# Turned weights moved in 2 KB runs and a newly planned order, in a four-layer graph stack on one core

## The chip, the cores and the metric

One core of a Trainium2 chip runs the kernel. The metric is device time in microseconds (us), the median of the timed runs; lower is better. Three runs of the kernel before took 3433.74, 3434.24 and 3435.35 us. The profile is of one further execution.

## The reference, cut to what matters

The input is `x` of 32 samples, each with 512 nodes and 256 channels, in float32, and one 512 x 512 adjacency matrix. Four layers follow one another, and after each one `x = layernorm(x + layer(x))`:

```
a: h = x W;  e = leaky(s1[i] + s2[j]);  softmax over neighbours;  elu(attention @ h)      one head
b: q, k, v;  8 heads of softmax(mask(q k^T)) @ v;  layernorm;  feed-forward;  layernorm
c: as a, with 4 heads of 64 channels
d: e = leaky((x W1)(x W2)^T);  masked softmax;  relu(attention @ (x W3))
```

All four build 512 x 512 attention weights row by row: the softmax runs along a row, with the node `i` on the partitions. To multiply them with the values they must be turned, so that the summed-over node `j` lies on the partitions. How they are turned for two heads of layer c is what the change is about.

## The kernel before, in words

Every sample is a graph of some 450 operations. `Plan.op` records an operation with its engine, its assumed duration, the buffers that it writes, reads and takes, and a stage name: the layer's letter and a digit (0 prepares, 1 makes scores and masks, 2 finishes the layer, 3 is softmax and turning, 4 is weighting). `Plan.order` then plans one instruction order for all engines: a list scheduler that holds up to four samples in flight (`WINDOW = 4`) and picks, for each free engine, the ready operation with the least key, `o.graph * AGE[e] - o.rank - URGENT[e].get(o.stage, 0)`. For TensorE the key gets `SWITCH_WEIGHT` times a penalty from the table `SWITCH`, for taking an operation of another form than the last one. The engines then run this order strictly, and semaphores hold them to the dependencies. So a change of `AGE`, `URGENT` or `SWITCH_WEIGHT` moves every instruction of the program and adds none.

TensorE has three forms of work. **Full**: matmuls and transposes on the whole 128 x 128 array. **Rows** (L934): the scores of layer b, four heads side by side, each on 32 of the array's rows. **Columns** (L603, in `weighted`): the weighting in b (four heads on 32 columns each) and in c (two heads on 64 columns each). A stretch of one form, from a change of form to the next, is called a run of that form below.

Each float32 matmul is two MATMUL records in the trace; a transpose is one. One group of four row heads is 8 records; one weighting of b is 32 records, one of c is 16.

Turning is done in two ways. In most places `turn` (L586) lets TensorE transpose four 128 x 128 blocks into a PSUM bank, which ScalarE or VectorE copies out (L529, L531) to a `pq` buffer. For heads 2 and 3 of layer c, in all but the last two samples (`BY_TRANSFERS`, `PLAIN`), TensorE is spared: the four row blocks of a head lie in one tile `tq`; VectorE transposes each 32 x 32 square in place (L702, STREAM_TRANSPOSE), and 16 transfers, issued by SyncE (SP) at L714, move the squares to their places in `pq`. Those are 60 heads, with 240 in-place transposes and 960 transfers of 64 KB. A transfer takes 32 partitions to 32 others, as 16 pieces of 32 floats (128 bytes) per partition. The other users of SP are the loads (L358) and the stores of the result (L1108).

Buffers are counted: 16 of `t` (one row block each), 2 of `tq`, 5 of `pq`, 8 PSUM banks.

Of the kernel before, what the change touches and what calls it, by code (L numbers as in the profile page):

```python
# [39 lines left out]
AGE = {"PE": 257, "ACT": 221, "DVE": -182, "POOL": 528, "SP": 151}  # L40
URGENT = {
    "PE": {"a0": -75, "a1": 707, "a2": 344, "b0": -756, "b1": 306, "b2": 700, "c0": -1085, "c1": -566, "c2": -26, "d0": -1544, "d1": -1472, "d2": -1512, "a3": 1865, "a4": 679, "b3": 269, "b4": -122, "c3": 3149, "c4": 468, "d3": -1054, "d4": 94},
    "ACT": {"a0": -877, "a1": 23, "a2": 412, "b0": 1122, "b1": 150, "b2": 22, "c0": 432, "c1": -809, "c2": -763, "d0": 680, "d1": -1928, "d2": -1182, "a3": 920, "a4": 701, "b3": 234, "b4": -604, "c3": 1629, "c4": 1505, "d3": -786, "d4": -337},
    "DVE": {"a0": 633, "a1": 670, "a2": 648, "b0": 1045, "b1": -236, "b2": -513, "c0": -2048, "c1": -657, "c2": 497, "d0": -1572, "d1": -869, "d2": -2025, "a3": 1551, "a4": 544, "b3": -1617, "b4": -331, "c3": 91, "c4": 1954, "d3": -1641, "d4": -1168},
    "POOL": {"a0": -1566, "a1": -815, "a2": 2482, "b0": 1576, "b1": -742, "b2": -986, "c0": -744, "c1": -1896, "c2": 3131, "d0": 1272, "d1": 1709, "d2": -1760, "a3": -1181, "a4": 746, "b3": -824, "b4": 1874, "c3": -105, "c4": 2168, "d3": 1794, "d4": 2316},
    "SP": {"a0": 578, "a1": -291, "a2": 1436, "b0": -478, "b1": -110, "b2": -662, "c0": -380, "c1": -1000, "c2": 35, "d0": 1115, "d1": -375, "d2": -249, "a3": 144, "a4": 71, "b3": -603, "b4": 627, "c3": -231, "c4": 1331, "d3": 989, "d4": -515},
# [6 lines left out]
SWITCH_WEIGHT = 869  # L53
# [18 lines left out]
class Buf:  # L72
# [13 lines left out]
    def place(self, tiles, words):  # L86
        if self.tag is None:
            self.view = self.pool.tile(self.shape, self.dtype, tag=self.name, name=self.name, bufs=1)
            return
        name = f"{self.tag}_{self.slot}"  # L90
        if name not in tiles:
            tiles[name] = self.pool.tile([self.shape[0], words], F32, tag=name, name=name, bufs=1)
        view = tiles[name][:, 0 : self.words()]
        if self.dtype != F32:
            view = view.bitcast(self.dtype)
        if len(self.shape) > 2:
            dims = " ".join("abc"[: len(self.shape) - 1])
            sizes = {k: n for k, n in zip("abc", self.shape[1:])}
            view = view.rearrange(f"p ({dims}) -> p {dims}", **sizes)
        self.view = view  # L100
# [210 lines left out]
def gnn_stack(  # L311
# [31 lines left out]
    def buf(tag, shape, name, cells=1, dtype=F32):  # L343
        return Buf(work, shape, tag, BUFS[tag], name, cells, dtype)
# [155 lines left out]
    class Rows:  # L500


        def __init__(self, buf, cell=None):
            self.buf, self.cell = buf, cell
            self.use = buf if cell is None else (buf, cell)

        def __call__(self):
            return self.buf[:] if self.cell is None else self.buf[:, self.cell]

    def rows(n, name, together=False):  # L510

        if together:
            t = buf("tq", [P, n, N], name, n)
            return [Rows(t, i) for i in range(n)]
        return [Rows(buf("t", [P, N], f"{name}_{i}")) for i in range(n)]
# [64 lines left out]
    def turn(t, pT, pcell, to, name):  # L580
# [3 lines left out]
        def issue(e):  # L584
            for j in range(NB):
                nc.tensor.transpose(ps[:, j], t()[:, block(j)], ident)  # L586

        op({PE: 0.44}, issue, [ps], [t.use], [pT])
        copied(N, to, lambda: ps[:], [(pT, pcell)], [ps])

    def weighted(pv, oT, pTs, of, v, lo, D, us):
# [4 lines left out]
        def issue(e):  # L596
            for j in range(NB):
                for h in range(P // D):
                    p = of(h, j)
                    at = pv[h * D : (h + 1) * D]  # L600
                    if len(p.shape) > 2:
                        at = at.rearrange("d (i n) -> d i n", n=P)
                    nc.tensor.matmul(  # L603
# [76 lines left out]
    def masked(s, t, top, i):  # L680


        def issue(e):
            nc.vector.tensor_tensor_reduce(  # L684
                out=t(), in0=s[:], in1=neg[:, i], scale=1.0, scalar=LOWEST, op0=ALU.add,
# [3 lines left out]
        op({DVE: 0.61}, issue, [t.use, (top, i)], [s, (neg, i)])  # L689

    def turned(ts, pT, blocks, by_transfers, name):


        if not by_transfers:
            for i in blocks:
# [3 lines left out]
            return  # L699

        for i in blocks:
            op({DVE: FLIP_US}, lambda e, t=ts[i]: nc.vector.transpose(t(), t()), [ts[i].use], [])  # L702
        t = ts[0].buf

        def squares():
            return t[:].rearrange("p i (j n) -> p (i j) n", n=P)

        for a in range(P // SQ):

            def move(e, a=a):  # L710
                here = slice(a * SQ, (a + 1) * SQ)
                for b in range(P // SQ):
                    there = slice(b * SQ, (b + 1) * SQ)
                    nc.sync.dma_start(out=pT[there, :, here], in_=squares()[here, :, there])  # L714

            op({SP: P // SQ * DMA_US}, move, [(pT, a)], [t], lag=2.0)

    def leaky_softmax(ts, top, v, src, total, at, blocks, name):
# [17 lines left out]
        for i in blocks:  # L736

            def leaky(e, i=i, t=ts[i]):
                nc.scalar.activation(  # L739
                    t(), t(), AF.Prelu, alpha=SLOPE,  # L740
# [3 lines left out]
            def exp(e, i=i, t=ts[i]):  # L744
                nc.scalar.activation(  # L745
                    t(), t(), AF.Exp, bias=bias[:, i : i + 1],
# [3 lines left out]
            op({ACT: 0.53 if src is None else 0.62}, leaky, [ts[i].use], [] if src is None else [v])  # L750
            op({ACT: 0.71}, exp, [ts[i].use, (total, at * NB + i)], [bias])
# [30 lines left out]
    class Gat(Layer):  # L782
# [31 lines left out]
        def attend(self):  # L814
            H, D, name, v = self.H, C // self.H, self.name, self.v
            G = min(H, P // D) if H > 1 else 1
            for g in range(0, H, G):
# [3 lines left out]
                for h in range(G):  # L821
                    plan.stage = name[0] + "1"
                    dst = bank([P, N], f"{name}_dst{g}{h}")
                    by_transfers = (
                        g + h in BY_TRANSFERS[name[0]] and int(name[1:]) < B - PLAIN
                    )
                    ts = rows(NB, f"{name}_t{g}{h}", by_transfers)
                    pT = buf("pq", [P, NB * NB, P], f"{name}_pT{g}{h}", NB)
# [8 lines left out]
                    o = op({PE: 0.44}, issue, [dst], [v], [t.buf for t in ts])  # L837
# [6 lines left out]
                    turned(ts, pT, range(NB), by_transfers, f"{name}_{g}{h}")  # L844
# [3 lines left out]
                if H > 1:  # L848
# [4 lines left out]
                        lambda h, j, pTs=pTs: pTs[h][:].rearrange(  # L853
                            "p (i j) n -> p i j n", j=NB
                        )[:, :, j],
# [34 lines left out]
    def rows_weighted(pv, pT, v, y, f):  # L890

        for i in range(FB):

            def issue(e, i=i):
                for j in range(NB):
                    nc.tensor.matmul(  # L896
                        pv[:, i], lhsT=pT[:, (f * FB + i) * NB + j], rhs=v[:, j, 0:C],
# [3 lines left out]
            reads = pT if BY_TRANSFERS[y.name[0]] else (pT, f * FB + i)  # L901
            op({PE: 1.73}, issue, [pv], [reads, v], [y])

    class Transformer(Layer):
# [14 lines left out]
        def attend(self):  # L919
            name, q_sb, k_sb = self.name, self.q, self.k  # L920
            for f in range(F):
# [4 lines left out]
                for c in range(NC):  # L926
                    ts = [rows(Q, f"{name}_t{f}{c}{i}") for i in range(FB)]
                    for i in range(FB):
                        ss = [bank([P, N], f"{name}_s{f}{c}{i}{q}") for q in range(Q)]

                        def scores(e, i=i, ss=ss, c=c, f=f):
# [8 lines left out]
                            {PE: 0.95}, scores, ss, [(q_sb, f), k_sb], [t.buf for t in ts[i]],  # L940
                            form="rows",
                        )
                        for q in range(Q):
# [3 lines left out]
                            def reduce(e, i=i, h=h, t=t, s=s, f=f, low=low):  # L947
                                nc.vector.tensor_tensor_reduce(  # L948
                                    out=t(), in0=s[:], in1=neg[:, f * FB + i],
# [4 lines left out]
                            def exp(e, i=i, h=h, t=t, low=low, total=total):  # L954
                                nc.scalar.activation(  # L955
                                    t(), t(), AF.Exp, bias=low[:, i, h : h + 1], scale=-1.0,
# [4 lines left out]
                            op({DVE: 0.61}, reduce, [t.use, (low, cell)], [s, (neg, f * FB + i)])  # L961
                            op({ACT: 0.71}, exp, [t.use, (total, cell)], [(low, cell)])

                    pTs = [
                        buf("pq", [P, 2 * NB, FN], f"{name}_pT{f}{c}{k}", 2 * FB)
                        for k in range(Q // 2)
                    ]
                    plan.stage = name[0] + "3"
                    for i in range(FB):
                        for q in range(Q):  # L970
                            pT, lo = pTs[q // 2], q % 2 * NB
                            turn(
                                ts[i][q], pT, q % 2 * FB + i,
                                lambda pT=pT, lo=lo, i=i: pT[:, lo : lo + NB, block(i)],
                                f"{name}_tr{f}{c}{i}{q}",
                            )
# [4 lines left out]
                        lambda h, j, pTs=pTs: pTs[h // 2][:, h % 2 * NB + j],  # L981
# [61 lines left out]
    class Bilinear(Layer):  # L1043
# [13 lines left out]
        def attend(self):  # L1057
            name, hh, xT = self.name, self.hh, self.xT
            ts = rows(NB, f"{name}_t", bool(BY_TRANSFERS["d"]))
            pT = buf("pq", [P, NB * NB, P], f"{name}_pT", NB)  # L1060
            top = tiny("top", [P, NB], f"{name}_top", NB)
            total = tiny("total", [P, NB, 1], f"{name}_total", NB)
            for f in range(F):
# [3 lines left out]
                for i in blocks:  # L1067
# [9 lines left out]
                    op({PE: 1.73}, issue, [s], [(hh, f), xT], [ts[i].buf])  # L1077
# [3 lines left out]
                turned(ts, pT, blocks, False, f"{name}_{f}")  # L1081
# [5 lines left out]
                plan.stage = name[0] + "4"  # L1087
                pv = bank([P, FB, C], f"{name}_pv{f}")
                y = self.part_y(f)
                rows_weighted(pv, pT, self.v, y, f)  # L1090

                def issue(e, y=y, pv=pv, inv=inv):
                    for i in range(FB):
                        nc.vector.tensor_scalar(
                            y[:, i], pv[:, i], inv[:, i], 0.0, ALU.mult, ALU.max
                        )

                op({DVE: 0.79}, issue, [y], [pv, inv])
                plan.stage = name[0] + "1"
                yield f  # L1100
# [97 lines left out]
```

## Time and profile before

| what | value | how to read it |
|---|---|---|
| timed runs | 3434.24 us median of 3 | device time |
| span of the profiled execution | 3429.9 us | first to last instruction; 4.3 us less than the median of the timed runs |
| TensorE (PE) busy | 3397.8 us, 99% | ends of matmuls are modelled, so busy is not peak |
| VectorE (DVE) busy | 2922.9 us, 85% | |
| ScalarE (ACT) busy | 2785.3 us, 81% | |
| GpSimd (POOL) busy | 854.4 us, 25% | |
| transfers through SP's queue | 563,456 packets, 117.98 MB | 16.0% of 16 DMA engines' span |
| granted TensorE clock | 0.999 of full speed | mean over the span |

The profile has a view by group of instructions (busy time, mean, idle time before), one of waits (who waited for whom), the chain of work that ended last (at each step: what released it, with its duration), a timeline, and a table of busy time by stretch. A line number in it is that of the kernel printed above.

### The profile page before, as it was taken

What the parts mean: (1) busy time and instruction counts of PE and PEld (TensorE: products, weight loads), DVE (VectorE), ACT (ScalarE), POOL (GpSimd) and SP (SyncE); (2) the same over time, 40 slices, a digit from 0 to 9 for tenths busy, and PEclk for the clock granted to TensorE, in tenths of its full rate; (3) what the DMA queues carried; (4) which work ended last, traced back from release to release, by engine and by line L of the source; (5) the groups of instructions that cost most, each with busy time, mean ns of one, the idle gap of its engine ahead of it and who ended that gap; (6) DMA issues with size and microseconds to landing.
All of it is one profiled execution on the core that took longest, in us unless ns stands there. A gap on an engine that the chain in (4) does not pass through costs nothing.

```text
span 3429.9 us, 65651 instructions
## 1 busy us (share of the span) xinstructions
PE 3397.8 (99%) x22744; PEld 2531.6 (74%) x22744; DVE 2922.9 (85%) x8645; ACT 2785.3 (81%) x6747; POOL 854.4 (25%) x840
## 2 busy tenths in 40 slices
PE   8999999999999999999999999999999999999998
PEld 6766777777777777777777777777777777777766
DVE  7889888888888888898888888888888889888886
ACT  6788788888788888888787888878888888878785
POOL 1222132222222222222223222222222222222322
PEclk9999999999999999999999999999999999999999
DMA  2012111121121220112211112102122011221100
GB/s 95 11 26 44 30 28 36 40 44 37 20 43 33 44 44 18 39 32 44 44 31 26 37 39 44 38 19 44 32 44 44 18 39 32 44 44 31 26 20 19
DMA packets 563787, 122.17 MB, mean 36 GB/s; under 512 B 510848, under 2 KB 562688, under 8 KB 563456
## 3 DMA queue, kind: packets, MB, share of 16 engines
q1 hardware_dynamic: 563456, 117.98, 16.0%
q8 instruction: 181, 2.97, 0.4%
q14 instruction: 150, 1.23, 0.1%
HBM read 38.21 MB, written 16.78 MB: 16 GB/s over the span
## 4 chain that ended last, share of the span: by engine, by line
PE 97%; ACT 1%; DVE 1%; DMA 1%; issue 0%; SPq 0%; POOL 0%; POOLq 0%; DVEq 0%; ACTq 0%
PE ps L586 21%; PE ps L603 14%; PE ps L896 13%; PE ps L557 13%; PE ps L572 10%; PE ps L934 8%; PE ps L806 7%; PE ps L1072 6%; PE ps L542 3%; PE ps L835 2%; PE ps L619 2%; ACT tq L745 0%; ACT t L739 0%; ACT pq L529 0%; DMA xT<-in_x_T 0%
## 5 line engine op out<-in xcount | busy, mean ns | idle before, releaser
L586 PEld LDWEIGHTS ps<-ident,t 128*128 128x128 f32 x6208 | 696.7, 141 | 221.7 <-ACT t L955 72.8
L955 ACT ACTIVATE t<-t,low 128x512 f32<-128x512 f32 x1024 | 737.5, 732 | 132.6 <-DVE low L948 132.6
L586 PE MATMUL ps<-ident,t 128*128 128x128 f32 x6208 | 824.2, 276 | 6.1 <-ACT t L745 5.5
L529 ACT COPY pq<-ps 128x512 f32<-128x512 f32 x1054 | 573.1, 588 | 240.6 <-PE ps L586 239.9
L676 POOL TENSOR_TENSOR y<-y,x 128x512 f32<-128x512 f32 x256 | 328.1, 1282 | 1563.3 <-DVE y L631 676.8
L948 DVE CUSTOM_DVE_ANT_0 t<-ps,neg 128x512 f32<-128x512 f32 x1024 | 646.2, 683 | 50.5 <-PE ps L934 50.2
L656 POOL TENSOR_TENSOR rstd<-rstd,mhalf 128x2 f32<-128x2 f32 x384 | 281.3, 733 | 843.3 <-DVE rstd L653 827.5
L603 PE MATMUL ps<-pq,v 128*32 128x256 f32 (+1 forms) x5120 | 490.2, 425 | 0.6 <-issue 0.4
L896 PE MATMUL ps<-v,pq 128*128 128x256 f32 x2048 | 473.4, 379 | 0.7 <-ACT pq L529 0.7
L896 PEld LDWEIGHTS ps<-v,pq 128*128 128x128 f32 x2048 | 377.1, 190 | 47.7 <-ACT pq L529 1.1
L603 PEld LDWEIGHTS ps<-pq,v 128*32 128x32 f32 (+1 forms) x5120 | 210.5, 115 | 254.9 <-issue 127.2
L531 DVE COPY pq<-ps 128x512 f32<-128x512 f32 x498 | 326.4, 678 | 56.2 <-PE ps L586 55.9
L745 ACT ACTIVATE t<-t,bias 128x512 f32<-128x512 f32 x528 | 373.5, 708 | 0.1
L684 DVE CUSTOM_DVE_ANT_0 t<-ps,neg 128x512 f32<-128x512 f32 x528 | 338.2, 681 | 15.5 <-PE ps L1072 11.2
L739 ACT ACTIVATE t<-t,v 128x512 f32<-128x512 f32 x400 | 271.8, 716 | 56.4 <-DVE top L684 54.1
L650 DVE BATCH_NORM_STATS2 st<-y 128x6 f32<-128x256 f32 x768 | 285.3, 413 | 9.6 <-POOL y L676 9.4
L934 PE MATMUL ps<-qk,qk 32*128 32x512 f32 x2048 | 283.4, 633 | 0.0
L557 PE MATMUL ps<-xT,w_qkv_sb 128*128 128x256 f32 x1024 | 236.2, 379 | 1.0 <-ACT t L739 1.0
L1072 PE MATMUL ps<-xT,qk 128*128 128x512 f32 x512 | 235.9, 593 | 0.0
L557 PEld LDWEIGHTS ps<-xT,w_qkv_sb 128*128 128x128 f32 x1024 | 192.0, 190 | 26.2 <-ACT t L739 1.4
L955 ACT ACTIVATION_READ_ACCUMULATOR t<-t,low 128x1 f32 x1024 | 209.4, 205 | 0.0
L739 ACT ACTIVATE tq<-tq,v 128x512 f32<-128x512 f32 x240 | 159.8, 717 | 42.5 <-DVE top L684 42.5
(93 smaller groups left out, 5195.2 us busy)
## 6 DMA issues: line engine op xcount, KB each, us to landing
pq<-tq SPq DMA_DIRECT2D x960, 64.0 KB, 2.1
xT<-in_x_T SPq DMA_DIRECT2D x64, 256.0 KB, 3.3
x<-in_x SPq DMA_DIRECT2D x32, 512.0 KB, 4.0
out<-y SPq DMA_DIRECT2D x64, 256.0 KB, 2.1
t<-in_adj SPq DMA_DIRECT2D x4, 256.0 KB, 6.0
w_qkv_sb<-in_L_gnn_w_qkv SPq DMA_DIRECT2D x1, 768.0 KB, 6.4
w_sb<-in_L_gnn_w SPq DMA_DIRECT2D x2, 256.0 KB, 5.6
t<-in_L_gnn_W SPq DMA_DIRECT2D x2, 256.0 KB, 2.7
```

Of the source, the lines that this page charges most:

```text
L529: nc.scalar.copy(dst(), ps())
L557: nc.tensor.matmul(ps[:, c], lhsT=w[:, k, lo + c * P : lo + (c + 1) * P], rhs=xT[:, k, nlo : nlo + FN], start=(k == 0), stop=(k == NC - 1),)
L572: nc.tensor.matmul(ps[:, i], lhsT=xT[:, k, nlo + i * P : nlo + (i + 1) * P], rhs=w[:, k, lo : lo + C], start=(k == 0), stop=(k == NC - 1),)
L586: nc.tensor.transpose(ps[:, j], t()[:, block(j)], ident)
L603: nc.tensor.matmul(at, lhsT=v[:, j, lo + h * D : lo + (h + 1) * D], rhs=p, start=(j == 0), stop=(j == NB - 1), skip_group_check=True,)
L739: nc.scalar.activation(t(), t(), AF.Prelu, alpha=SLOPE, bias=0.0 if src is None else v[:, i, src : src + 1],)
L745: nc.scalar.activation(t(), t(), AF.Exp, bias=bias[:, i : i + 1], accum_out=total[:, i, at : at + 1],)
L896: nc.tensor.matmul(pv[:, i], lhsT=pT[:, (f * FB + i) * NB + j], rhs=v[:, j, 0:C], start=(j == 0), stop=(j == NB - 1),)
L934: nc.tensor.matmul(s[:], lhsT=q_sb[at, c, block(f * FB + i)], rhs=k_sb[at, c], start=True, stop=True,)
L948: nc.vector.tensor_tensor_reduce(out=t(), in0=s[:], in1=neg[:, f * FB + i], scale=-1.0 / math.sqrt(D1), scalar=HIGHEST, op0=ALU.add, op1=A ...
L955: nc.scalar.activation(t(), t(), AF.Exp, bias=low[:, i, h : h + 1], scale=-1.0, accum_out=total[:, i, h : h + 1],)
L1072: nc.tensor.matmul(s[:], lhsT=hh[:, k, block(i)], rhs=xT[:, k], start=(k == 0), stop=(k == NC - 1),)
```

## The change

The two-way turning stays where it is, for the same heads of the same samples. What changes:

- The row blocks of those heads live in four ordinary `t` buffers until the softmax is done. VectorE's transpose then goes out of place, from `t` to `tq`, and writes the squares sorted by the partitions that they will go to: `tq` is `[128, 4 (b), 4 (m), 4 (j), 32]`. A transfer then reads one contiguous 2 KB run per partition (`tq[here, b]`) and writes one (`pT[.., a]`).
- The turned tile of such a head has the shape `[128, 4 (a), 4 (m), 4 (j), 32]`, so the weighting reads its 512 columns as 16 runs of 32 floats; before it read 4 runs of 128.
- In layer b the turned tile now has one layout for all users: the copies out of PSUM write 512 contiguous floats (before, 4 runs of 128), and the weighting reads 2 runs of 128 (before, 256 contiguous).
- The class `Rows` goes; layer d gets a path by squares that the settings do not use.
- `AGE`, `URGENT` and `SWITCH_WEIGHT` get new values, so that the whole order is planned anew.

```diff
-AGE = {"PE": 257, "ACT": 221, "DVE": -182, "POOL": 528, "SP": 151}
+AGE = {"PE": 322, "ACT": 299, "DVE": -131, "POOL": -1267, "SP": 901}
...
-SWITCH_WEIGHT = 869
+SWITCH_WEIGHT = -559
...
+    def columns(pT, m, j):
+        if len(pT.shape) == 5:
+            return pT[:, :, m, j].rearrange("p a m c -> p m a c")
+        return pT[:].rearrange("p (m j) n -> p m j n", j=NB)[:, m, j]
...
+    def into_squares(t, tq, m):
+        def issue(e):
+            nc.vector.transpose(tq[:, :, m].rearrange("p b j c -> p j b c"), t[:])
+        op({DVE: FLIP_US}, issue, [(tq, m)], [t])
+
+    def moved(tq, pT):
+        for a in range(P // SQ):
+            def move(e, a=a):
+                here = slice(a * SQ, (a + 1) * SQ)
+                for b in range(P // SQ):
+                    nc.sync.dma_start(
+                        out=pT[b * SQ : (b + 1) * SQ, a].rearrange("p m j c -> p (m j c)"),
+                        in_=tq[here, b].rearrange("p m j c -> p (m j c)"),
+                    )
+            op({SP: P // SQ * DMA_US}, move, [(pT, a)], [tq], lag=2.0)
...
-        for i in blocks:
-            op({DVE: FLIP_US}, lambda e, t=ts[i]: nc.vector.transpose(t(), t()), [ts[i].use], [])
-        t = ts[0].buf
-
-        def squares():
-            return t[:].rearrange("p i (j n) -> p (i j) n", n=P)
-
-        for a in range(P // SQ):
-            def move(e, a=a):
-                here = slice(a * SQ, (a + 1) * SQ)
-                for b in range(P // SQ):
-                    there = slice(b * SQ, (b + 1) * SQ)
-                    nc.sync.dma_start(out=pT[there, :, here], in_=squares()[here, :, there])
-
-            op({SP: P // SQ * DMA_US}, move, [(pT, a)], [t], lag=2.0)
```

The tables `URGENT`, one number per engine and stage, change throughout and are left out here.

## Prediction

> **What bounds the kernel now.** I read the page's shares first, then the busy time by stretch, then the chain of work that ended last, and at last the chain in one sample's length.
>
> ```profile
> PE 3397.8 (99%) x22744; PEld 2531.6 (74%) x22744; DVE 2922.9 (85%) x8645; ACT 2785.3 (81%) x6747; POOL 854.4 (25%) x840
> ...
> PE 97%; ACT 1%; DVE 1%; DMA 1%; issue 0%; SPq 0%; POOL 0%; POOLq 0%; DVEq 0%; ACTq 0%
> ...
> pq<-tq SPq DMA_DIRECT2D x960, 64.0 KB, 2.1
> ```
>
> TensorE (PE) is the bound: 99% busy, and 97% of the chain. The last row is what the change is named after; the chain has no step of it.
>
> ```profile
> 0.00:100.00 100.00, 87.94 (x590) 70.37 (x591) 74.33 (x213) 69.20 (x164) 16.40 (x24) 1.00 0.28 90
> 100.00:400.00 300.00, 292.26 (x2012) 217.02 (x2010) 256.53 (x747) 233.77 (x569) 75.33 (x73) 0.99 0.13 24
> 1449.00:1555.00 106.00, 106.00 (x714) 79.07 (x713) 91.24 (x273) 87.62 (x213) 26.61 (x26) 1.00 0.18 38
> 3240.00:3345.00 105.00, 103.42 (x715) 74.80 (x712) 90.33 (x265) 85.75 (x212) 23.95 (x24) 1.00 0.11 22
> 3345.00:3430.00 85.00, 74.15 (x365) 53.20 (x363) 56.80 (x168) 47.11 (x113) 20.15 (x20) 0.98 0.06 19
> ```
>
> Columns: stretch, its length, then busy us of PE, its weight loads, VectorE, ScalarE, GpSimd, the granted clock, DMA share and GB/s. In the steady state PE has no idle time at all; the other engines have 14% or more. All of PE's 32.1 us of idle time (3429.9 less 3397.8) lies in the ramps. So time can be lost or won by what PE itself does, and a little in the ramps. What PE does between the matmuls shows in the chain (start, us, line, records):
>
> ```profile
> 1481.10 1.93 PE ps L934 x16
> 1483.03 1.86 PE ps L603 x32
> ...
> 1488.10 1.07 PE ps L934 x8
> 1489.17 1.02 PE ps L586 x8
> ...
> 1491.51 3.58 PE ps L603 x16
> 1495.09 0.59 PE ps L586 x4
> 1495.68 0.44 PE ps L542 x4
> ...
> 1497.42 1.73 PE ps L557 x8
> ```
>
> These lines price a change of form. **Rows** (L934): one group takes 1.07, two in a row 1.93; so a group is 0.86 and each run of rows pays 0.21 besides. **Full**: four transposes take 0.44 inside a run, but 0.59 as the first after another form; eight take 1.02 where 2 x 0.44 would be 0.87 or 0.88: each full run pays 0.15. **Columns**: L603 x32 streams the columns of eight 256-column matmuls four abreast, for which L557 x8 takes 1.73; it takes 1.86: 0.13 a run. On 64 columns, x16 takes 3.58 where L557's rate gives 2 x 1.73 = 3.46: 0.12. The price is per run, whatever its length.
>
> **The change part by part.**
>
> *The new order* is the part with a price. The instruction order of the built programs can be counted; the work is the same (6208 transposes, 256 row groups, 128 + 64 column weightings, the same other matmuls), but it is cut up otherwise:
>
> | runs of one form on PE | before | after |
> |---|---|---|
> | full | 321 | 398 |
> | rows | 225 | 255 |
> | columns, 32 / 64 | 128 / 64 | 127 / 64 |
>
> Sum: 77 x 0.15 + 30 x 0.21 - 1 x 0.13 = 11.6 + 6.3 - 0.1 = **17.7 us more**. The cause can be read in the order: in the old one, 31 pairs of row groups stand together; in the new one, a single pair does. In the steady part two samples hold 20 full and 14 row runs before, 25 and 16 after: 5 x 0.15 + 2 x 0.21 = 1.2 us for two samples. PE has no idle time there to hide this in, so all of it reaches the end. The Trainium skill ("TensorEngine Tiling (Array Packing)", Key Properties) says that a change of tiling mode drains TensorE and a change of tile does not. That speaks against this order and names no price; by the rule alone all 106 new runs cost alike, while the rows above price the forms apart.
>
> *Copies* stay balanced: VectorE takes 511 of the `pq` copies after 498, ScalarE 1041 after 1054 (588 and 678 ns each in the rows), under 10 us on either engine in the whole span. Nothing, hidden by the 14% of slack.
>
> *Masks and softmax into `t` instead of `tq`*: the rows have the same means for both (681 and 683 ns on L684, 708 and 710 on L745). Nothing. The four `t` are given back at the transpose, and `tq` is held shorter; buffers were planned for.
>
> *Transposes out of place*: 240 of them, 685 ns in place. A gain has no reason: they move the same elements. From above the nearest row is the slowest VectorE form on 128 x 512, L884 with 842 ns: 8 x 0.16 = 1.3 us per sample on an engine with 14 us of slack in 106. I take 0 for the time, with 0 to 2 us in the ramps for the range.
>
> *The transfers*: 960 before and after, 64 KB each, with 32 pieces of 2 KB instead of 512 of 128 bytes. What they cost PE today is in the view of L714's waits: 0.6 us, one wait of L603. That is the most that faster transfers can give in this order. How much faster: 16 issues of 627 ns take 10.7 us for a head (one runs from 1544.71 to 1555.38), then 2.1 us to land. The nearest row with 2 KB runs, the stores at L1108, issues in 390 ns and lands in 2.1 us as well. So a head's transfers may shrink from 12.8 to about 9 us (16 x 0.43 + 2.1, an estimate from those rows). I take 0 in time; 0 to -0.6 for the range. The Trainium skill ("DMA: Bandwidth & Descriptors", Specifications) wants 512 bytes or more for line rate; its section "Why small descriptors are slow (HBM only)" exempts moves inside SBUF. The landing rows, 2.1 us at 128 bytes and at 2 KB, agree with the exemption at this size; by the first rule the DMA engines' 16.0% would fall, and the sum by either is the same, since PE does not wait for them.
>
> *The weighting's reads*: heads 2 and 3 now read 16 runs of 32 floats per 512 columns instead of 4 of 128. The trace has no such read. From below, 0: L603 on 32 columns reads contiguously and pays 0.13 a run, L603 on 64 columns reads four pieces and pays 0.12; breaks cost nothing visible. From above: were the whole 0.12 due to its 3 breaks in each of 16 records, a break would cost 2.5 ns, and 12 more in 16 records of 30 weightings would give 14 us. I take 0, nearest to the row. The two runs of 128 in layer b lie between the contiguous and the four-piece row: 0.
>
> Sum: 17.7 us on the profiled execution's 3429.9 gives 3447.6; the timed median lies 4.3 us above the span, so **3452.0 us**.
>
> **The rivals.**
>
> *A. The new order waits in the steady state.* PE works strictly in order, so a weighting whose `pq` is late holds up everything behind it, and with it the PSUM banks that ScalarE and VectorE drain. Adding up PE's work between the broadcast of head 3 (L835) and the weighting of heads 2 and 3 gives 38 us in every sample before; in the new order 46 and 26 by turns. Against: head 3's squares took 9 to 15 us from the broadcast at 1454.29 to their last transposes (1463.66 for the third, 1469.14 for the fourth), then 10.7 for the issues and 1.5 more to land: 22 to 27 us. So 26 is at the edge, and with issues as short as the stores' it is enough. For: the other head took 17.3 us (1527.33 to 1544.65), and 29.5 against 26.2 would be 3.3 us in 15 samples, 50 us. A middle case of about 1 us gives 3452 + 15 = **3467**.
>
> *B. Not slower: the new order waits less.* It decides if it wins back 17.7 us. In the ramps, of 32.1 us idle, 10.7 is the wait for the first weights and 1.2 for `xT` (both orders begin alike), 8.1 follows the last matmul: about 12 us are open. In the steady state, start-to-start times above the prices leave some 0.7 us per sample, 20 us in 28 samples. Winning half of these 32 gives 3452 - 16 = **3436**, no difference that shows; all of them 3420. For it: a new order is free to fill the ramps otherwise. Against: more changes of form fill nothing, and the two ends look much alike in the two orders.
>
> *C. A new access form is slow.* If the weighting's short runs cost 14 us as bounded above, or the transposes hold VectorE up, **3466** and more. That the change does not do what it says is no rival here: the order lists show `32x512` transfers in place of `32x16x32`.
>
> **How the numbers follow.** The forecast, the runs' price alone: 0.62. A: 0.17; B: 0.15 (of which 0.03 beyond -7 us); C: 0.06. A measurement of this kernel can tell about 0.2%, 7 us, from no change: below 3427.4 is faster, above 3441.1 slower. Slower 0.62 + 0.17 + 0.06 = 0.85, same 0.12, faster 0.03. The range runs from 3440 (two thirds of what B needs) to 3470 (A's middle case and C's bound).
>
> **What would show it.** PE runs at 99% with a longer span; two samples take 1.2 us more than the 210.9 of now (twice 105.43, the distance of the same piece in the chain); L586's first pieces of 0.59 grow in number; L603 x16 stays at 3.58 (C wrong) or not; no DMA or STREAM_TRANSPOSE in PE's waits (A wrong) or a wait of a us or more ahead of L639 on every second sample (A right). SP's issues fall towards 0.4 us with no effect on the end. I am wrong if the ramps shrink by ten us or more, or if a form change costs less in the new surroundings.

## The result, and the profile after

The changed kernel takes **3440.39 us** (median of 16 runs, 3438.95 to 3442.79) where the kernel before takes 3433.6 in the same comparison (16 runs, 3431.29 to 3435.35): a ratio of 1.0020, 95% interval 1.0013 to 1.0028. So it is 6.8 us slower. The forecast was 17.7 us slower: the sign is right, the amount is not.

The page of the changed kernel first, with the shares of the engines, SP's transfers, the chain, and the row of the moved squares:

```profile
PE 3406.7 (99%) x22744; PEld 2510.1 (73%) x22744; DVE 2971.2 (86%) x8673; ACT 2778.5 (81%) x6719; POOL 863.3 (25%) x840
...
q1 hardware_dynamic: 102656, 117.98, 12.2%
...
PE 96%; DVE 2%; ACT 1%; DMA 1%; SPq 0%; issue 0%; POOL 0%; POOLq 0%; DVEq 0%; ACTq 0%
...
pq<-tq SPq DMA_DIRECT2D x960, 64.0 KB, 2.0
```

The change does what it says: the same bytes go in 102,656 packets where there were 563,456. The chain is TensorE as before. Three rows of the busy times by stretch of the changed kernel (columns as in the prediction):

```profile
100.00:400.00 300.00, 298.79 (x2046) 221.34 (x2045) 266.77 (x780) 246.50 (x599) 80.43 (x78) 1.00 0.09 24
1449.00:1555.00 106.00, 105.99 (x722) 76.54 (x722) 91.91 (x266) 89.08 (x217) 24.52 (x24) 1.00 0.17 46
...
3345.00:3437.00 92.00, 77.07 (x383) 53.64 (x381) 60.79 (x180) 53.03 (x127) 20.25 (x20) 0.98 0.05 18
```

The row to look at is the first. From 100 to 400 us TensorE was idle for 7.7 us before, and is idle for 1.2 now, with 34 more records done (2046 after 2012). Before, four waits that end at 200.4, 262.9, 378.8 and 386.1 us make 6.7 us of it: three for ScalarE in the softmax, one for a layernorm. The changed order has one wait of 0.9 us there. The start is better than it was; the rest has to be worse by more.

Busy time cannot say by how much, since the ends of matmuls are modelled (a transpose is shown for some 275 ns, and the next one starts after 109) and a short wait lies under the matmul ahead of it. So I went by **starts**. A run of one form lasts from its first start to the first start of the next run. From that I took its work (109 ns for each transpose, 215 and 429 ns for 256 and 512 columns, the spacings inside runs, rounded here, and 859 ns for a row group) and the price of the run by form (0.155 us full, 0.211 rows, 0.14 and 0.15 columns). What is left counts as waits. The sum closes on the span by construction; the split is mine, not a view of the profile. In us, for every kernel below (head is ahead of the first matmul; the last 8.1 to 8.5 us, behind the last one, are left out, and so is the work, 3237.3 in all):

| kernel | span | head | runs: price | waits to 400 us | waits between | waits in the last 230 us |
|---|---|---|---|---|---|---|
| before | 3429.9 | 10.7 | 738: 124.8 | 18.9 | 21.0 | 9.1 |
| changed | 3437.2 | 10.3 | 844: 142.9 | 7.4 | 18.6 | 12.4 |
| e1_old_layout | 3442.9 | 10.4 | 844: 142.9 | 8.1 | 22.4 | 13.6 |
| e2_new_path_old_weights | 3534.5 | 10.4 | 741: 125.2 | 22.6 | 120.5 | 10.3 |
| e3_old_path_new_weights | 3576.0 | 10.3 | 832: 141.0 | 22.1 | 137.5 | 19.6 |
| e4_apart | 3465.6 | 10.5 | 800: 136.1 | 22.6 | 41.5 | 9.4 |
| e5_loads_first | 3436.2 | 10.5 | 844: 142.9 | 7.7 | 16.2 | 13.5 |
| e6_dummy_rows | 3441.4 | 10.4 | 802: 136.5 | 20.5 | 19.5 | 9.0 |
| e7_priced | 3426.5 | 10.0 | 731: 123.3 | 11.3 | 27.3 | 9.1 |
| e8_priced_more_runs | 3516.9 | 10.2 | 798: 135.6 | 11.4 | 102.4 | 11.9 |
| e9_priced_loads_first | 3426.9 | 10.0 | 731: 123.3 | 10.3 | 28.8 | 8.7 |
| e10_priced_old_layout | 3447.6 | 10.3 | 731: 123.3 | 10.4 | 47.5 | 10.6 |

Changed less before: +18.1 price, -11.5 waits in the first ramp, -2.4 between, +3.3 at the end, -0.4 head, which makes 7.1; the spans differ by 7.3.

The price in this sum is counted, not measured: the number of runs times the prices of the kernel before. The chain of the changed kernel has pieces of the same length (start, us, line, records):

```profile
1484.53 1.07 PE ps L953 x8
...
1492.70 1.86 PE ps L639 x32
1494.56 1.02 PE ps L620 x8
...
3335.22 3.58 PE ps L639 x16
```

What is called waits holds lost clock too. In the kernel before, TensorE stood idle for 2.73 us up to 200.4 us, and then 16 transposes took 3.53 us, 213 ns apart instead of 109. The timeline, and the row by stretch, in which the third number from the end is the granted clock:

```profile
200.42 3.53 PE L586 MATMUL ps<-ident,t 128*128 128x128 f32 x16 [2.73 <-ACT t L745]
```

```profile
200.60:204.00 3.40, 3.40 (x17) 2.91 (x17) 3.24 (x8) 2.85 (x9) 0.00 (x0) 0.51 0.34 58
```

So 3.4 us ran at half the clock, which lost 1.7. The changed kernel's trace has no such stretch before its last matmul: of the 11.5 us, 9.8 are waits and 1.7 is clock that was lost behind a wait. In e2, e3 and e8 the traces have 34, 61 and 41 us at half the clock, so up to 17, 31 and 20 us of what stands as waits there.

So the **theory** after the result: the price of the runs is real and is 18 us; the new order gives most of it back in the first 400 us, once. **Rivals**: the price is smaller than read from the chain (then nothing was given back); or the layout of the transfers, and not the order, moved the time.

### The profile page after: what moved, and what is told of

It reads as the page before. It is cut to its first block, busy times and chain, and to the rows that moved or that the text cites. A ratio compares the mean times of both kernels' runs of the same rounds, so it can differ in the third digit from the quotient of the medians.

```text
span 3437.2 us, 66007 instructions
## 1 busy us (share of the span) xinstructions
PE 3406.7 (99%) x22744; PEld 2510.1 (73%) x22744; DVE 2971.2 (86%) x8673; ACT 2778.5 (81%) x6719; POOL 863.3 (25%) x840
## 2 busy tenths in 40 slices
DMA packets 102990, 122.19 MB, mean 36 GB/s; under 512 B 19328, under 2 KB 71168, under 8 KB 102656
## 3 DMA queue, kind: packets, MB, share of 16 engines
q1 hardware_dynamic: 102656, 117.98, 12.2%
q14 instruction: 153, 1.25, 0.1%
## 4 chain that ended last, share of the span: by engine, by line
PE 96%; DVE 2%; ACT 1%; DMA 1%; SPq 0%; issue 0%; POOL 0%; POOLq 0%; DVEq 0%; ACTq 0%
PE ps L620 20%; PE ps L639 13%; PE ps L915 13%; PE ps L591 13%; PE ps L606 9%; PE ps L953 8%; PE ps L828 7%; PE ps L1102 7%; PE ps L576 3%; PE ps L856 2%; PE ps L655 2%; DMA xT<-in_x_T 0%; ACT t L761 0%; DVE t L720 0%; DVE st L686 0%; DVE pq L565 0%
## 5 line engine op out<-in xcount | busy, mean ns | idle before, releaser
L620 PE MATMUL ps<-ident,t 128*128 128x128 f32 x6208 | 814.7, 275 | 2.7 <-ACT t L767 2.0
L712 POOL TENSOR_TENSOR y<-y,x 128x512 f32<-128x512 f32 x256 | 342.5, 1348 | 1586.9 <-DVE y L903 701.9
L967 DVE CUSTOM_DVE_ANT_0 t<-ps,neg 128x512 f32<-128x512 f32 x1024 | 652.1, 686 | 99.5 <-PE ps L953 95.9
L720 DVE CUSTOM_DVE_ANT_0 t<-ps,neg 128x512 f32<-128x512 f32 x768 | 494.0, 683 | 75.3 <-PE ps L1102 40.7
L767 ACT ACTIVATE t<-t,bias 128x512 f32<-128x512 f32 x768 | 543.2, 709 | 1.0
L639 PE MATMUL ps<-pq,v 128*32 128x256 f32 (+1 forms) x5120 | 481.9, 425 | 0.0
L915 PE MATMUL ps<-v,pq 128*128 128x256 f32 x2048 | 464.8, 380 | 0.0
L761 ACT ACTIVATE t<-t,v 128x512 f32<-128x512 f32 x640 | 421.8, 716 | 27.6 <-DVE top L720 21.8
L915 PEld LDWEIGHTS ps<-v,pq 128*128 128x128 f32 x2048 | 381.4, 190 | 59.6 <-DVE y L667 10.6
L565 DVE COPY pq<-ps 128x512 f32<-128x512 f32 x511 | 337.2, 683 | 46.0 <-PE ps L620 44.4
L639 PEld LDWEIGHTS ps<-pq,v 128*32 128x32 f32 (+1 forms) x5120 | 189.7, 115 | 241.7 <-issue 124.2
L953 PE MATMUL ps<-qk,qk 32*128 32x512 f32 x2048 | 297.2, 639 | 0.0
L532 DVE STREAM_TRANSPOSE tq<-t 128x512 f32<-128x512 f32 x240 | 163.4, 697 | 6.3 <-ACT t L767 6.2
```

The source lines that it names most:

```text
L620: nc.tensor.transpose(ps[:, j], t[:, block(j)], ident)
L639: nc.tensor.matmul(at, lhsT=v[:, j, lo + h * D : lo + (h + 1) * D], rhs=p, start=(j == 0), stop=(j == NB - 1), skip_group_check=True,)
L720: nc.vector.tensor_tensor_reduce(out=t[:], in0=s[:], in1=neg[:, i], scale=1.0, scalar=LOWEST, op0=ALU.add, op1=ALU.max, accum_out=top[:, i ...
L761: nc.scalar.activation(t[:], t[:], AF.Prelu, alpha=SLOPE, bias=0.0 if src is None else v[:, i, src : src + 1],)
L767: nc.scalar.activation(t[:], t[:], AF.Exp, bias=bias[:, i : i + 1], accum_out=total[:, i, at : at + 1],)
L915: nc.tensor.matmul(pv[:, i], lhsT=stationary(pT, f * FB + i, j), rhs=v[:, j, 0:C], start=(j == 0), stop=(j == NB - 1),)
```

## The experiments

### Is the price of a run real? e6_dummy_rows and e4_apart

`e6_dummy_rows` is the kernel before with one tiny row matmul (counted as no work above) ahead of layer a's transposes, once per sample. It splits a full run, so that 32 row runs and 32 full runs are added; the output is not touched.

```diff
+                        if H == 1:
+                            nc.tensor.matmul(
+                                dst[:, 0:8], lhsT=ident[0:32, :], rhs=ident[0:32, 0:8], start=True, stop=True
+                            )
```

> The kernel before, with one extra matmul of 32 rows on 8 columns ahead of the first transpose of layer a in each sample, into the bank that the transposes then overwrite: it adds no wait and next to no work, but cuts a full run in two, 32 times (32 more row runs, 32 more full runs). Theory (0.15 for a full run, 0.21 for a run of rows): 32 x 0.37 = 11.7 us and about 1 us for the matmul itself, 3445 to 3447 us. Rival (a change of form is cheaper when little stands in the run): 3437 to 3440 us.

Measured: 3444.5 us (3443.07 to 3445.3), ratio 1.0033, interval 1.002 to 1.0045; 11.45 us above the kernel before. The added matmul in the trace of e6 (minimum, median and maximum in ns):

```profile
L834 PE MATMUL ps<-ident x64: 251/262/272, 18.0 to 3209.1; 32*128 32x8 f32 x64
```

It has next to no work of its own (eight columns), so what it costs is nearly all the change to rows and back: 11.45 / 32 = 0.36 us, as 0.21 + 0.15 from the chain of before. By the account the waits of e6 add up to 49.0 us as those of the kernel before do, and all that is added is price. That the two sums are equal to the tenth is luck: e6's first ramp has a second stretch at half clock (at 265.7 us, 1.7 us), and its waits between are 1.5 less. The price stands, in the old order, and the first rival falls.

`e4_apart` makes changes of form in the old order: of the 31 places where two row groups stand together, the full operation ahead of them goes between them.

```diff
+        if (y.form, r1.form, r2.form) != ("full", "rows", "rows"):
+            continue
+        i, k = out.index((y, "PE")), out.index((r1, "PE"))
...
+        out.insert(k + 1, out[i])
+        del out[i]
```

> The kernel before, and in its order the 31 pairs of row groups that stand together are taken apart: the full operation ahead of a pair goes between its two groups, nothing else moves. 352 full and 256 row runs instead of 321 and 225. Theory (price per run 0.15 and 0.21): 31 x 0.36 = 11.2 us more than the kernel before, 3445 us. Rival (a change of form costs less than the single lines say, and the sum of 17.7 was too high for that reason): 3439 us or less.

Measured: 3468.13 us, ratio 1.0101 (1.0087 to 1.0115): +35 us, three times what was expected. The chain of e4 around one of the 31 places (start, us):

```profile
1496.53 1.22 PE ps L948 x8
1497.74 0.59 PE ps L600 x4
1498.33 1.84 PE ps L948 x8
```

The full operation between the two row groups has its usual 0.59. The second row group takes 1.84 where a single one takes 1.07: a wait of 0.77 that the list of TensorE's matmuls does not show. Each row group takes four of the eight PSUM banks, and in this kernel the moved operation writes a bank that the second group needs next, so that group waits until ScalarE or VectorE has copied it out. At this place ScalarE's copy runs from 1498.41 to 1499.00, and the group's last two weight loads (PEld) follow it:

```profile
1499.05 0.29 PEld L948 LDWEIGHTS ps<-qk,qk 32*128 32x128 f32 x2 [0.48 <-ACT pq L543]
```

31 x 0.77 = 24 us, with 11.3 of price, is the 35 us. So e4 was no clean test of the price: it added a wait that neither theory had in it. It does say something of the change: to pull row groups apart one has to plan the banks with it. In the new order, which has all but one pair apart, none of the 254 single row groups takes over 1.4 us from start to start.

### Order or data path? e2_new_path_old_weights and e3_old_path_new_weights

Each takes one half of the change: e2 the new data path with the planner's old weights (`AGE`, `URGENT`, `SWITCH_WEIGHT`), e3 the old path with the new weights.

```diff
-AGE = {"PE": 322, "ACT": 299, "DVE": -131, "POOL": -1267, "SP": 901}
+AGE = {"PE": 257, "ACT": 221, "DVE": -182, "POOL": 528, "SP": 151}
...
-SWITCH_WEIGHT = -559
+SWITCH_WEIGHT = 869
```

> The changed data path planned with the old AGE, URGENT and SWITCH_WEIGHT: 741 runs of one form instead of 738 (324 full, 225 rows, 128 and 64 columns). Theory: 3 x 0.15 = 0.5 us of price, and the old waits in the first ramp: 3434 us, 3431 to 3437. Rival (the 2 KB runs save time by themselves): 3423 us.

> The old data path (in place, runs of 128 bytes) planned with the new weights: 832 runs (387 full, 254 rows, 127 and 64 columns), a price of 66 x 0.15 + 29 x 0.21 = 16 us above the kernel before. Theory, with the first ramp set by the weights and shorter by some 10 us: 3440 us, 3436 to 3445. Rival (the shorter ramp came with the data path): 3450 us, with some 7 us of idle TensorE between 100 and 400 us as before.

Measured: e2 3533.68 us, ratio 1.0292 (1.0278 to 1.0306); e3 3573.35, ratio 1.0407 (1.0393 to 1.0421). Both expectations failed by some 100 us. The counts of runs were as expected (741 and 832); the waits were not. The two costliest waits of TensorE in e2, and then in e3 (us in total, times, longest):

```profile
PE ps L591 <- ACT xT L563: 24.5, 29, 0.9
PE ps L576 <- DVE x L700: 24.1, 28, 0.9
```

```profile
PE ps L603 <- DMA pq<-tq: 22.1, 14, 2.2
PE ps L586 <- ACT t L955: 16.4, 12, 2.3
```

In e2 two waits recur in nearly every sample; in e3 the weighting stands before transfers that are late, rival A's wait in an order that was not planned for it. The weights are fitted to one graph of operations and one set of durations; with another graph they give another order and a poor one. So these two do not split the change into halves, as I had meant them to. They do show that the short first ramp belongs to neither half alone: 22.6 and 22.1 us of waits to 400 us, against 18.9 before and 7.4 in the changed kernel.

### The same order, old layout: e1_old_layout

This one does split it: the changed kernel's operations in its order, instruction for instruction, with the squares unsorted, so that a transfer again moves 128-byte pieces and the weighting reads 4 runs of 128.

```diff
-            nc.vector.transpose(tq[:, :, m].rearrange("p b j c -> p j b c"), t[:])
+            nc.vector.transpose(tq[:, m], t[:])
...
-                    nc.sync.dma_start(
-                        out=pT[b * SQ : (b + 1) * SQ, a].rearrange("p m j c -> p (m j c)"),
-                        in_=tq[here, b].rearrange("p m j c -> p (m j c)"),
-                    )
+                    there = slice(b * SQ, (b + 1) * SQ)
+                    squares = tq[:].rearrange("p i (j n) -> p (i j) n", n=P)
+                    nc.sync.dma_start(out=pT[there, :, here], in_=squares[here, :, there])
```

> The changed kernel with its order kept instruction for instruction (844 runs of one form on TensorE), but with the old layout: squares unsorted, transfers in runs of 128 bytes, the weighting reading 4 runs of 128. Theory (the order alone made the time: more changes of form, less waiting in the first 400 us): 3440 us, within 2 of the changed kernel. Rival (the 2 KB runs won back the missing 11 us of the 17.7): 3446 to 3451 us. Rival C (the short reads of the weighting cost something that the ramps hid): below 3438.

Measured: 3444.87 us (3443.03 to 3448.36), ratio 1.0036 (1.0023 to 1.0049); the median is 4.5 us above the changed kernel's, the span 5.7 us, of which 1.1 stand in a stretch of 6.8 us at half clock near the end that the changed kernel's trace lacks. The two ratios' intervals overlap a little, but with equal orders the two traces can be laid on each other matmul by matmul, and of the steps over 0.15 us between them +3.2 us stand at one place, layer a's first matmuls (L828 in the changed kernel, L827 in e1). What they wait for, in the changed kernel, in e1, and in e5 (below):

```profile
PE ps L828 <- DMA xT<-in_x_T: 2.7, 2, 1.4
```

```profile
PE ps L827 <- DMA xT<-in_x_T: 3.9, 5, 1.6
```

```profile
PE ps L851 <- DMA xT<-in_x_T: 0.4, 1, 0.4
```

SP's timeline ahead of one such place, in the changed kernel:

```profile
816.35 2.41 SPq L544 DMA_DIRECT2D pq<-tq  x4
...
819.49 2.41 SPq L544 DMA_DIRECT2D pq<-tq  x4
821.95 1.12 SPq L358 DMA_DIRECT2D xT<-in_x_T  x2
```

And in e1:

```profile
817.96 2.61 SPq L546 DMA_DIRECT2D pq<-tq  x4
...
821.27 2.63 SPq L546 DMA_DIRECT2D pq<-tq  x4
823.95 1.14 SPq L358 DMA_DIRECT2D xT<-in_x_T  x2
```

The loads of `xT` are issued behind eight transfers, four of which take 2.4 us to issue with 2 KB pieces and 2.6 with 128 bytes, and TensorE needs `xT` at about 825.5 in the changed kernel. The layout does count, then, but for the most part through SP's queue and by a load that stands behind the transfers. I had put it at 0 to -0.6 us, from the waits of the old order.

### Is it SP's queue? e5_loads_first

The changed kernel, with the loads of `xT` moved ahead of up to five entries of SP's queue where their buffer is already free.

```diff
+        while passed < 5 and out[j - 1][0].n not in need and not (out[j - 1][1] == "SP" and out[j - 1][0].stage == "a0"):
+            j -= 1
+            passed += out[j][1] == "SP"
+        if j < i:
+            out.insert(j, out.pop(i))
...
-    order = plan.order()
+    order = sooner(plan.order())
```

> The changed kernel; on SP alone the loads of xT are moved ahead of up to five queue entries (transfers and stores) where their buffer is free; nothing else moves. Theory (in the new order the load of xT lands just as TensorE needs it, and the transfers ahead of it on SP set when it is issued): the waits ahead of L828 go, 2 to 5 us, so 3436 to 3438 us. Rival (TensorE does not wait for the load, the difference between the old and the new layout lies elsewhere): 3440 us as the changed kernel.

Measured: 3437.99 us (3436.77 to 3439.55), ratio 1.0014 (1.0005 to 1.0023). The wait goes from 2.7 to 0.4 us (the third line above), the waits between the ramps from 18.6 to 16.2, and the median is 2.4 us below the changed kernel's (1.9 when each is taken against the kernel before in its own comparison). The intervals of the two ratios overlap; the wait's disappearance is what shows the cause.

### Where is the order won and lost? eight_before and eight_after

Both kernels on the first eight samples alone; the other 24 are left out. If the new order wins in the first ramp and pays per sample, it must win here.

```diff
-    B, N, C = x.shape
+    B, N, C = 8, x.shape[1], x.shape[2]
```

> The kernel before on the first 8 samples alone (24 samples of work are left out): its ramps and some four samples of steady state. 3433.6 less 24 x 105.43 us is 903 us.

> The changed kernel on the first 8 samples alone. Its price of runs is 3.7 us above that of the old order (208 runs, 186 before). Theory (the new order loses in the steady state and wins in the first ramp: waits of 18.9 us there before, 7.4 after, and 3 more at the end): 903 + 3.7 - 11.5 + 3 = 898 us, faster than the kernel before on 8 samples. Rival (the 6.8 us are spread evenly over the samples): 903 + 1.7 = 905 us, slower.

Measured: 900.93 us (899.31 to 902.05) in the old order and **897.02** (896.46 to 897.26) in the new one: the order that loses 6.8 us on 32 samples wins 3.9 on eight, (6.8 + 3.9) / 24 = 0.45 us per sample lost between. The stretch from 100 to 400 us, old order and then new:

```profile
100.00:400.00 300.00, 292.60 (x2017) 217.38 (x2016) 257.18 (x748) 233.80 (x569) 75.24 (x73) 0.99 0.13 24
```

```profile
100.00:400.00 300.00, 298.79 (x2048) 221.39 (x2044) 266.76 (x780) 246.33 (x599) 80.84 (x79) 1.00 0.09 24
```

The same picture as with 32 samples. By starts, the waits of the first 400 us are 18.2 and 7.2 us; the price is 31.5 (186 runs) and 35.2 us (208 runs).

### Fewer changes of form and a short ramp together: e7, e8, e9

If price and ramp are separate, an order can have both. For e7 and e8 the planner of the changed kernel got the measured prices and weights chosen to go with them; no operation changes.

```diff
-SWITCH = {"full": {"rows": 0.1, "columns": 0.1}, "rows": {"full": 0.12, "columns": 0.12}, "columns": {}}
-SWITCH_WEIGHT = -559
+SWITCH = {"full": {"rows": 0.21, "columns": 0.14}, "rows": {"full": 0.155, "columns": 0.14}, "columns": {"full": 0.155, "rows": 0.21}}
+SWITCH_WEIGHT = 2882
...
-                            {PE: 0.95}, scores, ss, [(q_sb, f), k_sb], ts[i],
+                            {PE: 0.86}, scores, ss, [(q_sb, f), k_sb], ts[i],
```

> The changed kernel's data path, planned anew: the planner's prices of a change of form are set to those that the trace shows (0.21 us for a run of 32-row matmuls, 0.155 for a full run, 0.14 for a 32-column run), its prices of three matmul groups to the measured ones (0.86, 1.724 and 3.44 us), and the weights of its rules chosen to go with them. Every operation is the same; only the order differs. Its TensorE list has 731 runs (322 full, 218 row, 191 column) instead of the changed kernel's 844 (378 full, 275 row, 191 column). Theory (the changed kernel pays 18 us more for changes of form and gets back 11.5 us of waits in the first 400 us; the two are separate): the price is 123.3 us, 19.6 less than the changed kernel's; with the waits of the changed kernel the time is about 3420 us, 13 below the kernel before. Rival 1 (fewer changes of form and short waits in the ramps exclude each other): the waits of the first 400 us go back to about 19 us, and the time is about 3432 us, as before. Rival 2 (the order waits in the steady state, since the planner's other figures are rough): above 3440 us.

> As the run with 731 runs, with another choice of the planner's weights, whose TensorE list has 798 runs (355 full, 252 row, 191 column), 46 fewer than the changed kernel's. Theory: 7.3 us less price than the changed kernel, so with its waits about 3432 us; 12.3 us above the run with 731 runs. Rivals: as there, plus or minus the waits of its own order; if the time is at or below that of the run with 731 runs, the number of changes of form isn't what tells the two apart.

> The kernel with 731 runs, and on SP the loads of xT moved ahead of up to 5 entries of the queue where their buffer is free, as was done with the changed kernel, where it took 2.4 us off. Theory: takes away what layer a's first project waits for the load of xT, 0 to 3 us less than without it. Rival: the transfers that the load passes are late for a weighting in this order, and the time is the same or longer.

(In the first of these the changed kernel's 844 runs are split wrongly; it has 398 full and 255 row runs, as in the prediction's table. The price, 142.9 us, is that of the right split.)

Measured: e7 **3429.41** us (3428.27 to 3431.03), ratio 0.9990 (0.9981 to 0.9999), 3.0 us faster than the kernel before and, with e9, the fastest here; e8 3519.27, ratio 1.0250 (1.0236 to 1.0264); e9 3430.23, ratio 0.9992 (0.9983 to 1.0001).

For e7 the price came off as reckoned (by the account, which counts it), and a good part of the short ramp stayed (11.3 us of waits, neither the 7.4 of the changed kernel nor the 18.9 of the old). What the expectation missed are 8.7 us more waits between the ramps: 3429 and not 3420. The kernel e8 has 46 runs fewer than the changed kernel and is 79 us slower; the second rival of its expectation. The first of TensorE's waits in e8 (not counting the one for the weights at the start):

```profile
PE ps L587 <- DVE nT L561: 52.3, 23, 2.3
```

Of these 23 waits, of some 2.27 us each, nine are followed by 3.4 us at half clock. So the count of runs prices an order only where the waits are equal; it does not tell a good order from a bad one. The kernel e9 does not differ from e7: the order of e7 waits only 0.4 us for `xT`, so there was next to nothing to take away.

### The layout in the best order: e10_priced_old_layout

The order of e7, instruction for instruction, with the edit of e1: squares unsorted, 128-byte pieces.

> The kernel with 731 runs, its order kept instruction for instruction, but the squares unsorted again: transfers of 128-byte pieces, and the weighting reads 4 runs of 128. Theory (the old layout cost the changed kernel's order 4.5 us only because there the loads of xT stand right behind 8 transfers on SP and reach TensorE too late; it isn't the layout that makes TensorE faster): in the order with 731 runs TensorE waits only 0.4 us for xT, so the old layout costs 0 to 2 us, about 3430 us. Rival (shorter pieces cost by themselves, wherever the loads stand): 4 us or more, 3433 to 3435 us.

Measured: 3450.29 us (3449.41 to 3455.91), ratio 1.0052 (1.0039 to 1.0066). Both answers were far too low: the old layout costs this order **21 us**, in time and in span (3447.6 less 3426.5), or 19.5 us when each is taken against the kernel before in its own comparison. Laid on e7's trace matmul by matmul, 19.0 us of it stand ahead of the weighting of the transferred heads and 2.9 at layer a's first matmuls. TensorE's waits in e10:

```profile
PE ps L634 <- DMA pq<-tq: 4.1, 5, 1.5
PE ps L823 <- DMA xT<-in_x_T: 3.7, 4, 1.6
```

and the end of a row of transfers in e10's chain, with the weighting that waits for it:

```profile
1792.04 0.63 SPq L542
...
1792.72 2.99 DMA pq<-tq
1795.70 0.35 issue
1796.05 5.48 PE ps L634 x46
```

Now SP's issues stand in the chain, ahead of TensorE: this is rival A of the prediction, with its wait and its place. The same 24 transfers on SP's timeline, in e7 and in e10:

```profile
1769.85 15.86 SPq L540 DMA_DIRECT2D pq<-tq  x24
```

```profile
1776.23 17.11 SPq L542 DMA_DIRECT2D pq<-tq  x24
```

In e7 the last issue ends at 1785.71, lands at 1787.11, and the weighting starts at 1787.46 without a wait; there is little to spare. In e10 the issues take 1.25 us longer and the weighting stands. This recurs at some 13 weightings, for 0.7 to 2.5 us each. What TensorE's own list of waits shows (4.1 us) is a fifth of it; the rest is seen from start to start. One reason shows in another of these weightings. It takes two heads side by side, and in e10 the last transfer of the second head lands at 1158.58, after the weighting's first two records:

```profile
1158.72 4.62 PE L634 MATMUL ps<-pq,v 128*64 128x512 f32 x30 [0.38 <-DMA pq<-tq]
```

In e7 the first two records start 0.01 us apart, and so do the last two; here the first two start 0.48 us apart and the last two 0.43 us, so the heads run alone there. The weighting lasts 5.00 us from start to start instead of 3.58, of which the list has 0.38.

## Why the prediction was right or wrong, by its steps

- **The sum of the runs, 17.7 us: right, as far as it could be measured.** e6 shows the price by itself, in the old order: 11.45 us for 32 + 32 runs. In the changed kernel 18.1 us is a count at those prices. Two samples take 211.77 us in the steady state, 0.9 more than 210.86; 1.2 was predicted.
- **"All of PE's 32.1 us of idle time lies in the ramps ... time can be lost or won by what PE itself does, and a little in the ramps": the step that failed.** I took the ramps' worth from idle time, and held it at before's level. In the first 400 us idle time was 12.1 + 7.7 us, 9.1 without the wait for the first weights; the waits from start to start were 18.9. The new order takes 11.5 of them away, 1.7 of it clock that was lost behind a wait. "The two ends look much alike in the two orders" was a look at the list of instructions, which has no waits in it. Rival B had this mechanism, and the prediction gave it 0.15; it reckoned that it takes 16 us for 3436. In all 11.0 us were won back (11.5 in the first ramp); ten us was the prediction's own sign of being wrong, and the two ramps together shrank by 8.2. The measured 3440.39 us lies at the very end of the range, an end that was worked out from rival B and not from the forecast's mechanism.
- **The transfers, 0 to -0.6 us: wrong in size, by being read from the old order.** In the changed kernel's order the old layout costs 4.5 us (e1), in e7's order 21 (e10). Without the new layout the change would have cost 12.0 us (3444.87 less 3432.83 in e1's comparison). Nor was 0.6 us "the most" in the old order: it came from the list of waits, and by starts five weightings of the kernel before (at 964, 1702, 2440, 2546 and 3284 us) last 3.75 to 4.39 us instead of 3.58, 2.2 us together. The estimate that a 2 KB transfer issues in about 0.4 us was wrong too: the median is 588 ns after 627.
- The end, held alike, lost 3.3 us, which pays back a part. Together: 18.1 - 11.5 - 2.4 + 3.3 - 0.4 = 7.1. Of the order alone (e1 less before): 18.1 of price, -10.8 in the first ramp, +1.4 between, +4.5 at the end (1.1 of it half clock).
- **Rival A** did not happen in the changed kernel: nobody waits for L544 in its trace, and outside the ramps its weightings on 64 columns keep their 3.58 us. It was no idle thought: it is what e10, and in part e3, are made of.
- **Rival C** did not happen: the weighting's short reads cost nothing (L639 on 64 columns takes 3.58 us a run as L603 did; e1, with long reads, is not faster), and the transposes out of place take 697 ns after 685.
- The copies, and masks and softmax into `t`: nothing seen of them on the path.

What stays open: why the new order's first ramp is shorter was shown by place and size, and four of the old waits are named above, but which moved operation took them away was not traced; the price was measured by itself in the old order only; and the new layout in the old order, instruction for instruction, was not run, so the 0 to -0.6 us is untested where it was meant.

## What to carry to other kernels

Where an engine shows 99% busy and its ends are modelled, go by its starts: work per record, price per change of form, and what is left is waits; idle time showed half of them here, and some of what looks like a wait is clock. Value a change of layout in the order in which it will stand: the same edit was worth some 5 us in one order and 21 in another, since a list of waits only tells what the present order had left uncovered. And an order planned for one graph is not to be carried to another: half of this change alone cost 100 and 140 us.

## What the runs showed of the hardware

- A transfer of 64 KB between 32 and 32 partitions takes SP 588 ns to issue (median) as 32 pieces of 2 KB and 627 ns as 512 pieces of 128 bytes, and lands in 2.0 and 2.1 us. The Trainium skill ("DMA: Bandwidth & Descriptors", "Why small descriptors are slow (HBM only)") exempts moves inside SBUF from its rule on small pieces; the landing times agree with that. The issue differs by 39 ns, and 24 issues in a row by 1.25 us; in e10 TensorE waits behind them.
- A row matmul of 32 rows and eight columns costs 0.36 us with the change of form there and back, nearly all of it the change.
- Two row groups with another operation between them: a wait of 0.77 us for a PSUM bank lay inside the second group's stretch of the chain (1.84 us after 1.07). The list of waits of TensorE's matmuls does not have it; that of its weight loads has part of it, 15.1 us in 32 waits for ScalarE's copy (e4), where the kernel before has 6.8 in 31.
- After idle time TensorE ran at half its clock for 3.41 us (6.83 in some places), but not every time: after 2.73 us of idle time in the kernel before; after nine of the 23 waits of 2.27 us in e8; at about 201 us after 2.23 us in e7 and not after 2.22 in e10.
